# Deformable convolution on one core: window weights of upper and lower tokens stored a chunk apart in DRAM, and the last two such layers in one loop over sixteen images

## The chip, the core and the metric

The kernel runs on one core of one Trainium2 chip. The core has TensorE (PE, with a queue of its own for loading weights, PEld), VectorE (DVE), ScalarE (ACT), GpSimd (POOL) and SyncE (SP), which here issues all DMA transfers; sixteen DMA engines move the data. The metric is the device time of one execution in microseconds (us), lower is better. One execution before and one after are also profiled; every line of a profile shown here is from such an execution.

## The reference

A network of four layers over x with 8 images of 56 x 56 tokens and 128 channels, all fp32. Layers 0, 2 and 3 are deformable convolutions (DCN), each with its own weights; layer 1 is a scan over the tokens in four directions (VSS), which the change doesn't touch. A DCN layer is

```python
xp = x @ w_in + b_in
h = depthwise_conv3x3(x); h = gelu(batch_norm(h))
offset = (h @ w_off + b_off).reshape(N, H, W, GROUP, P, 2)      # GROUP = 4, P = 9
mask = softmax((h @ w_msk + b_msk).reshape(N, H, W, GROUP, P), axis=-1)
# bilinear samples of xp at 9 displaced points, a set for each group of 32 channels,
# added up with the mask as weights
y = dcn_core(xp, offset, mask) @ w_out + b_out
x = x + gamma1 * layer_norm(y, ln1_g, ln1_b)
m = gelu(x @ w_fc1 + b_fc1) @ w_fc2 + b_fc2
x = x + gamma2 * layer_norm(m, ln2_g, ln2_b)
```

## The kernel before

The sampling has no gather. The displacements of a point over one image lie in a narrow range, so all that a token samples lies in a window of fixed size around it: 14 x 11 positions in layer 0, 12 x 10 in layer 2, 15 x 14 in layer 3 (rows x columns). For each token and group of channels the kernel works out one weight for each position of the window (bilinear weight times mask, added up over the nine points), and the sampling is then a product of a matrix of weights with the rows of xp.

An image is cut into 4 row blocks of 14 rows (`rb`), each of these into 7 blocks of 14 rows x 8 columns (`q`), 112 tokens each: 28 blocks an image, 224 a layer. A layer's loop (`Dcn.loop`) goes over the blocks in order and runs several streams side by side:

- `front` makes an image ready in 43 steps: `xt` is loaded and transposed on PE (L598), xp is made (L609, added up at L610) and stored in DRAM, and from there copied into `table`, where the positions of a column of blocks with its margins (`PC` wide) lie in a row; the depthwise convolution (L631), offsets and mask (`om`), softmax, the smallest displacement of each point, which gives the addresses of L745.
- `weigh` makes the weights of a row block, two groups of channels at a time. ACT makes `hat` (Abs at L727, Relu at L729, one Abs a tap), POOL multiplies by the mask (`ay`, L733) and clears `win` (L736, four buffers), DVE makes `patch` for three points (L742, one instruction) and adds it into `win` at an address held in a register (L745, three instructions). A group's `win` (112 tokens x 7 blocks x window) is then stored to the DRAM buffer `skew`, of which there are three (`SETS`).
- `fetch` loads a block, two blocks ahead of its use. A token's weights lie in `skew` by the position in its own window, and tokens are `SA` floats apart; read with a stride of `SA - 1` between neighbouring tokens, and with `8*SA - PC` between rows, each token's weights land at their position in the block's common window. So one transfer `sw` (L755) brings, for each of the 112 tokens, one row of four groups x `SLEN` positions, zeros outside the token's own window included. The block's rows of `table` come as `xw` (L757).
- `sample` turns `sw` chunk by chunk: the `SLEN` positions are `NJ` chunks of `KP`. PE transposes the four groups of a chunk (L769) into PSUM, ACT copies them to SBUF (`st`, L771), and PE multiplies by `xw` (`products`, L780): a matmul for each group into its 32 rows of the sum `yps`. The products of a chunk are issued two chunks behind its transposes (`LAG`). In a chunk at the end of the window only the upper (0 to 63) or lower tokens (64 to 111) have anything, and only these are transposed.
- `close` copies a finished half row block to `yT` (L790). `tail`, a few steps after each block, does w_out (L804), the norms (L839 on), fc1 (L822) and fc2 (L831), with the bias as a bf16 matmul that opens the sum (L556).

The geometry of the layers:

| | layer 0 | layer 2 | layer 3 |
|---|---|---|---|
| NJ chunks x KP positions = SLEN | 4 x 128 = 512 | 4 x 112 = 448 | 5 x 120 = 600 |
| tokens turned in each chunk | 112, 112, 64, 48 | 112, 112, 56, 48 | 112, 112, 96, 48, 48 |
| SA (floats from token to token) | 2048 | 1792 | 2400 |
| floats stored for a token and group | 252 | 204 | 315 |

Order: everything that goes over a DMA queue is issued by SP in program order. Stores are put on a list (`store`) and issued behind the next `fetch` (`flush`, L568). The streams are moved on by counts in `ahead`: the next image's front is spread over 28 blocks, the weights run 6 blocks and a row block ahead.

`run` does one layer: it opens the pools, loads the layer's weights and constants (`constants`, `split_bias`), and runs the loop. The loop of the first layer starts with its first image's front and the first row block's weights, before any block; so does the loop of each later one, since a layer's loop ends with its last tail before the next one's constants. Among the steps of that first front each layer clears its DRAM buffers and their margins (`zeros`).

The pools of PSUM hold three banks for the transposes, two for `yps` and three for the rest.

Of the kernel before, what the change touches and what calls it, by code (L numbers as in the profile page):

```python
# [61 lines left out]
BR, BC = 14, 8  # L62
# [12 lines left out]

class Geo:


    def __init__(self, y0, wy, x0, wx, kx, ky):
        self.Y0, self.WY, self.X0, self.WX = y0, wy, x0, wx  # L80

        self.PC, self.HR = BC + wx - 1, 14 * -(-(H + wy - 1) // 14)
        m = (BR + wy - 1) * self.PC
        self.NJ = -(-m // 128)
        self.KP = 8 * -(-m // self.NJ // 8)
        if self.KP % 16 and self.KP != 120:
            self.KP += 8
        self.SLEN = self.NJ * self.KP

        self.chunks = []  # L90
        for j in range(self.NJ):
            top, last = j * self.KP // self.PC, ((j + 1) * self.KP - 1) // self.PC
            t0, t1 = BC * max(0, top - wy + 1), BC * min(BR, last + 1)
            self.chunks.append((j, 64 if t0 >= 64 else 0, t1))
        self.chunks.sort(key=lambda chunk: (chunk[1], -chunk[2]))
        assert self.chunks[0][1:] == (0, TB)

        self.SA = G * self.SLEN
        self.WPAD = -(-(wy * self.PC + wx - kx) // 4) * 4
# [7 lines left out]
GEO = {0: Geo(-6, 14, -6, 11, *PATCH[0]), 2: Geo(-6, 12, -5, 10, *PATCH[2]), 3: Geo(-8, 15, -7, 14, *PATCH[3])}  # L107
# [36 lines left out]
class Net:  # L144
    def __init__(self, tc, ctx, d):
# [16 lines left out]
        most = max(geo.SA for geo in GEO.values())  # L162
        self.zeros = dram("zeros", [TB, most])
        self.padded = [dram(f"padded{k}", tab) for k in range(2)]
        self.table = {x: [dram(f"table{x}{k}", [NCB * geo.HR * geo.PC + 16, C]) for k in range(3)] for x, geo in GEO.items()}
# [307 lines left out]

class Dcn:


    def __init__(self, net, layer, images, src, dst):
        self.net, self.tc, self.nc, self.d = net, net.tc, net.nc, net.d
        self.layer, self.images, self.src, self.dst = layer, images, src, dst
        self.geo = GEO[layer]  # L480
        self.KX, self.KY = PATCH[layer]
        self.table, self.skew = net.table[layer], net.skew[layer]

    def run(self):
        tc, nc = self.tc, self.nc
        with ExitStack() as ctx:
# [10 lines left out]
            self.w = self.net.dcn_weights(self.layer, self.const)  # L497
            self.constants()
            self.split_bias()
# [3 lines left out]
        with tc.If(over > 0):  # L503
            self.net.dcn_slow(self.layer, self.images, self.src, self.dst)
# [4 lines left out]
    def constants(self):  # L509
        nc, d = self.nc, self.d  # L510
        self.taps = self.const("taps", [128, 10])
        nc.sync.dma_start(out=self.taps, in_=d["c_taps"].partition_broadcast(128))
        self.lim = self.const("lim", [2 * NS, 3])
        nc.sync.dma_start(out=self.lim, in_=d[f"c_lim{self.layer}"])
        self.over = self.const("over", [2 * NS, 2])
        nc.vector.memset(self.over, 0.0)
        self.b_in = self.const("b_in_all", [128, 128])
        nc.sync.dma_start(out=self.b_in, in_=d[f"w{self.layer}_row"][0, :128].partition_broadcast(128))
        self.b_om = self.const("b_om_all", [128, OM])
        nc.sync.dma_start(out=self.b_om, in_=d[f"w{self.layer}_row"][0, 384:].partition_broadcast(128))  # L520
        pat = self.const("pat_all", [128, 2 * NS])
        nc.sync.dma_start(out=pat, in_=d["c_pat"].partition_broadcast(128))
        nc.vector.tensor_add(self.b_om[:, : 2 * NS], self.b_om[:, : 2 * NS], pat)
        self.pad = self.img.tile([128, (H + 2) * WP], F32, name="pad", tag="pad")
        nc.vector.memset(self.pad, 0.0)

# [12 lines left out]
    def split_bias(self):  # L539

        nc = self.nc
        self.ones = self.const("ones3", [3, TB], BF16)
        nc.vector.memset(self.ones, 1.0)
        self.terms = self.const("terms", [3, 2, 128], BF16)
        rest = self.w["row"][:, 128:384]
        for k in range(3):
            term = self.const(f"term{k}", [1, 256], BF16)
            nc.vector.tensor_copy(term, rest)
            nc.sync.dma_start(out=self.terms[k : k + 1].rearrange("p i c -> p (i c)"), in_=term)
            less = self.const(f"rest{k}", [1, 256])  # L550
            nc.vector.tensor_sub(less, rest, term)
            rest = less

    def bias(self, ps, i, t):

        self.nc.tensor.matmul(ps[:TB, : t * 128].rearrange("p (t c) -> p t c", c=128), lhsT=self.ones, rhs=bcast(self.terms[:, i], 1, t), start=True, stop=False)  # L556
# [13 lines left out]
    def slot(self, x, g=None, q=None):  # L570

        t, geo = self.skew[x % SETS], self.geo
        if q is None:
            return bass.AP(tensor=t.tensor, offset=t.offset + g * geo.SLEN, ap=[[geo.SA, TB], [TB * geo.SA, NCB], [1, geo.WY * geo.PC]])
# [4 lines left out]
    def front(self, i):  # L579
        nc, w, n, geo = self.nc, self.w, TB, self.geo  # L580
# [5 lines left out]
        def load(rb):  # L586
            xt = self.fp.tile([128, NT, C], F32, name="xt", tag="xt", bufs=2)
            self.last = nc.sync.dma_start(out=xt[:n], in_=self.rows_of(self.src[i], rb))
# [4 lines left out]
        for rb in range(NRB):  # L593
# [12 lines left out]
            for t0, t1 in HALVES:  # L606
# [3 lines left out]
                nc.vector.tensor_add(xp[:n, t0:t1, :], ps[:n, : 128 * (t1 - t0)].rearrange("p (t c) -> p t c", c=C), bcast(self.b_in[:n], 1, t1 - t0))  # L610
# [12 lines left out]
        for rb in range(NRB):  # L623
# [14 lines left out]
            for t0, t1 in HALVES:  # L638
# [3 lines left out]
                nc.vector.tensor_add(om[:n, NCB * rb + t0 : NCB * rb + t1, :], ps[:n, : OM * (t1 - t0)].rearrange("p (t f) -> p t f", f=OM), bcast(self.b_om[:n], 1, t1 - t0))  # L642
# [34 lines left out]
        nc.vector.tensor_scalar(base, lo, self.lim[:, 0:1], self.lim[:, 1:2], ALU.max, ALU.min)  # L677
# [7 lines left out]
        nc.vector.tensor_sub(hi, hi, self.lim[:, 2:3])  # L685
# [15 lines left out]
    def windows(self, i, c, rb=None):  # L701

        t, geo = self.table[i % 3], self.geo
# [4 lines left out]
        return t[at : at + geo.SLEN].rearrange("(j p) c -> p j c", j=geo.NJ)  # L708
# [3 lines left out]
    def weigh(self, i, rb):  # L712

        nc, n, KX, KY, geo = self.nc, TB, self.KX, self.KY, self.geo
        K, GP = max(KX, KY), 2 * NP
# [6 lines left out]
        for gg in range(0, G, 2):  # L722

            hat = self.up.tile([128, GP, NCB, 2, K], F32, name="hat", tag="hat")
# [6 lines left out]
            ay = self.up.tile([128, GP, NCB, KY], F32, name="ay", tag="ay")  # L731
            yield
            nc.gpsimd.tensor_mul(ay[:n], hat[:n, :, :, 1, :KY], bcast(m, 3, KY))  # L733
            for g in (gg, gg + 1):
                win = self.up.tile([128, NCB, geo.WPAD], F32, name="win", tag="win", bufs=4)
# [10 lines left out]
                self.store(self.slot(NRB * i + rb, g=g), win[:n, :, : geo.WY * geo.PC])  # L746
# [4 lines left out]
    def fetch(self, i, rb, q):  # L751

        nc, n, geo = self.nc, TB, self.geo
        sw = self.bp.tile([128, G, geo.SLEN], F32, name="sw", tag="sw")
        nc.sync.dma_start(out=sw[:n].rearrange("p g m -> p (g m)"), in_=self.slot(NRB * i + rb, q=q))  # L755
        xw = self.bp.tile([128, geo.NJ, C], F32, name="xw", tag="xw")
# [4 lines left out]
    def sample(self, i, rb, q, yps):  # L761

        nc, KP = self.nc, self.geo.KP
        sw, xw = self.here.pop((i, rb, q))
        for at, (j, t0, t1) in enumerate(self.geo.chunks):
            n = t1 - t0
            ps = self.pt.tile([128, 512], F32, name="pt", tag="pt")
            for g in range(G):
                last = nc.tensor.transpose(ps[:KP, n * g : n * (g + 1)], sw[t0:t1, g, KP * j : KP * (j + 1)], self.net.ident[t0:t1, t0:t1])  # L769
            st = self.bp.tile([128, G * TB], F32, name="st", tag="st", bufs=4)  # L770
            nc.scalar.copy(st[:KP, : G * n], ps[:KP, : G * n])  # L771
            self.behind.append(partial(self.products, yps, xw, st, at))
            self.catch_up(LAG, last)

    def products(self, yps, xw, st, at):
        KP = self.geo.KP
        j, t0, t1 = self.geo.chunks[at]
        n = t1 - t0
        for g in range(G):
            self.nc.tensor.matmul(yps[CG * g : CG * (g + 1), t0:t1], lhsT=xw[:KP, j, CG * g : CG * (g + 1)], rhs=st[:KP, n * g : n * (g + 1)], start=at == 0, stop=at == self.geo.NJ - 1)  # L780
# [15 lines left out]
    def tail(self, i, rb, yT, X):  # L796
        nc, w, n, net = self.nc, self.w, TB, self.net
        yT = yT.rearrange("p (n t) -> p t n", t=NT)
        parts = []
        for t0, t1 in HALVES:  # L800
            po = self.psum()
            self.bias(po, 0, t1 - t0)
# [8 lines left out]
        for t0, t1 in HALVES:  # L811
# [16 lines left out]
            self.bias(po, 1, t1 - t0)  # L828
# [7 lines left out]
        self.store(self.rows_of(self.dst[i], rb), X[:n])  # L836
# [28 lines left out]
    def loop(self):  # L865
# [4 lines left out]
        rows = [(i, rb) for i in range(self.images) for rb in range(NRB)]  # L870
# [17 lines left out]
        if self.layer not in self.net.clean:  # L888
            margins = partial(self.net.clear_margins, after=lambda: self.last)
            weights = partial(self.net.clear_weights, self.layer, after=lambda: self.last)  # L890
            zeros = {0: [margins(0)], 12: [weights(0), margins(1)], 18: [weights(1)], 42: [weights(2)]}
# [13 lines left out]
        for at, (i, rb, q) in enumerate(order):  # L905
            if q == 0:
                X = self.tp.tile([128, NT, C], F32, name="X", tag="X", bufs=3)
                nc.sync.dma_start(out=X[:TB], in_=self.rows_of(self.src[i], rb))
# [5 lines left out]
            self.sample(i, rb, q, yps[:, TB * (q - t0) : TB * (q - t0 + 1)])  # L914
# [10 lines left out]
    def all_fronts(self):  # L925

        for i in range(1, self.images):
# [494 lines left out]
def tile_net(tc, d, out, images=NIMG, layers=(0, 1, 2, 3)):  # L1422
    with ExitStack() as ctx:
        net = Net(tc, ctx, d)
        src = d["x"]
# [69 lines left out]
```

## Time and profile before

| | |
|---|---|
| median of 8 runs | 18,874.83 us (18,837.58 to 18,891.82) |
| the profiled execution, its own time and span | 18,866.81 us, span 18,865.0 us |
| granted clock of TensorE, mean | 0.802 of full speed |
| busy share of the span | PE 76%, PEld 36%, DVE 81%, ACT 60%, POOL 62% |
| layer 0, first to last block's first L769 | 170.2 to 2145.1 us |
| layer 1 | about 2160 to 14,190 us |
| layer 2, the same | 14,330.1 to 16,129.0 us |
| layer 3, the same | 16,353.1 to 18,815.8 us |
| `sw` in layers 0, 2, 3 | 896, 784, 1050 KB a block, 224 blocks each |
| L769 (transposes of `sw`) | 11,648 instructions, 1915.1 us busy, mean 302 ns of one |
| L780 (products) | 23,296 records, 1224.6 us busy, mean 296 ns |

A fp32 matmul of L780 leaves two records in the trace, a transpose of L769 one. An instruction's mean is its own duration; matmuls are pipelined, so that the distance from one's start to the next one's is shorter. In a view by stretches, "(x...)" is the number of instructions, PEclk the granted clock in that stretch and "DMA share" the mean busy share of the sixteen DMA engines. In the timeline a row is a group of like instructions with its start, busy time, and in brackets the idle time of its engine before it, with what ended that.

### The profile page before, as it was taken

What the parts mean: (1) busy time and instruction counts of PE and PEld (TensorE: products, weight loads), DVE (VectorE), ACT (ScalarE), POOL (GpSimd) and SP (SyncE); (2) the same over time, 40 slices, a digit from 0 to 9 for tenths busy, and PEclk for the clock granted to TensorE, in tenths of its full rate; (3) what the DMA queues carried; (4) which work ended last, traced back from release to release, by engine and by line L of the source; (5) the groups of instructions that cost most, each with busy time, mean ns of one, the idle gap of its engine ahead of it and who ended that gap; (6) DMA issues with size and microseconds to landing.
All of it is one profiled execution on the core that took longest, in us unless ns stands there. A gap on an engine that the chain in (4) does not pass through costs nothing. (4 is left out here: it accounts for less than half of the span.)

```text
span 18865.0 us, 237115 instructions
## 1 busy us (share of the span) xinstructions
PE 14384.4 (76%) x79747; PEld 6872.4 (36%) x79747; DVE 15318.8 (81%) x18794; ACT 11224.8 (60%) x21363; POOL 11727.3 (62%) x6462
## 2 busy tenths in 40 slices
PE   6888787678778778778778778777666888577777
PEld 4555422222222222222222222222224666455555
DVE  7777379988988988988988889888966777677776
ACT  4665555566656656666656656656554666455555
POOL 1121079988988989989989989988961122111111
PEclk6777788889888888888888888888876777666767
DMA  8888544444433333334333333333326888587777
GB/s 239 232 219 217 133 155 159 163 157 152 144 142 141 143 142 140 141 143 145 140 144 137 146 144 140 140 145 133 140 101 167 217 214 213 155 207 211 207 212 179
DMA packets 1250535, 3112.19 MB, mean 165 GB/s; under 512 B 76608, under 2 KB 868180, under 8 KB 1181468
## 3 DMA queue, kind: packets, MB, share of 16 engines
q1 hardware_dynamic: 1249292, 3096.75, 52.8%
q8 instruction: 641, 10.50, 0.2%
q14 instruction: 602, 4.93, 0.1%
HBM read 2400.54 MB, written 872.17 MB: 173 GB/s over the span
## 5 line engine op out<-in xcount | busy, mean ns | idle before, releaser
L1405 POOL TENSOR_TENSOR hc<-h,bc 128x784 f32<-128x784 f32 x4096 | 7554.4, 1872 | 1023.1 <-DVE h L1400 801.2
L1400 DVE TENSOR_TENSOR_SCAN h<-dA,st,u 128x784 f32<-128x784 f32 x3072 | 5579.0, 1839 | 384.7 <-ACT dA L1299 268.7
L1299 ACT ACTIVATE dA<-dt,v_A 128x784 f32<-128x784 f32 x4096 | 3750.0, 917 | 792.6 <-DVE h L1400 788.9
L1331 PE MATMUL acc<-hc,v_sum 128*32 128x392 f32 x16384 | 3406.9, 565 | 85.0 <-POOL hc L1405 84.7
L1309 DVE TENSOR_TENSOR u<-dtu,bc 128x784 f32<-128x784 f32 x3072 | 2887.5, 958 | 592.1 <-PE dtu L1293 475.0
L1293 PE MATMUL dtu<-dt,ident 128*128 128x392 f32 x4096 | 2091.4, 637 | 1339.9 <-issue 940.3
L769 PE MATMUL pt<-ident,sw 112*128 112x112 f32 (+8 forms) x11648 | 1915.1, 302 | 467.1 <-DMA sw<-skew 458.9
L736 POOL MEMSET win<- 128x1820 f32 (+2 forms) x384 | 631.2, 1648 | 2461.0 <-DMA skew<-win 2033.1
L1400 DVE TENSOR_TENSOR_SCAN h<-dA,st,up 128x784 f32<-128x784 f32 x1024 | 1879.9, 1836 | 260.8 <-POOL hc L1405 134.3
L771 ACT COPY st<-pt 128x448 f32<-128x448 f32 (+6 forms) x2912 | 1233.0, 444 | 1325.0 <-PE pt L769 1283.3
L1305 POOL TENSOR_TENSOR up<-dt,bc 128x784 f32<-128x784 f32 x1024 | 1905.6, 1861 | 37.5 <-DVE h L1400 30.8
L1403 ACT COPY st<-h 128x1 f32<-128x1 f32 x3072 | 584.5, 190 | 2247.8 <-DVE h L1400 2239.0
L733 POOL TENSOR_TENSOR ay<-hat,om 112x756 f32<-112x756 f32 (+2 forms) x192 | 437.3, 2278 | 2166.7 <-ACT hat L729 1905.8
L1331 PEld LDWEIGHTS acc<-hc,v_sum 128*32 128x32 f32 x16384 | 802.6, 120 | 2598.7 <-issue 1705.5
L1293 PEld LDWEIGHTS dtu<-dt,ident 128*128 128x128 f32 x4096 | 852.5, 232 | 2401.2 <-issue 1472.2
L769 PEld LDWEIGHTS pt<-ident,sw 112*128 112x128 f32 (+8 forms) x11648 | 1343.3, 172 | 1049.1 <-issue 688.4
L745 DVE TENSOR_TENSOR win<-win,patch 112x252 f32 (+2 forms) x3456 | 1574.5, 466 | 55.4 <-DVE bn_st L847 15.1
L742 DVE TENSOR_TENSOR patch<-ay,hat 112x756 f32<-112x756 f32 (+2 forms) x1152 | 1221.5, 1074 | 444.9 <-POOL ay L733 444.6
L780 PE MATMUL yps<-st,xw 120*32 120x48 f32 (+8 forms) x23296 | 1224.6, 296 | 226.9 <-ACT st L771 189.1
L1069 PE MATMUL misc<-xn,v_tap 128*128 128x448 f32 x2016 | 879.8, 581 | 117.2 <-ACT xn L1103 61.2
L822 PE MATMUL ps<-xT,w_fc 128*128 128x448 f32 (+1 forms) x1536 | 797.1, 653 | 112.6 <-ACT xT L817 74.2
L1342 ACT COPY y<-acc 64x392 f32<-64x392 f32 x768 | 577.6, 752 | 446.2 <-PE acc L1331 436.4
(163 smaller groups left out, 19396.6 us busy)
## 6 DMA issues: line engine op xcount, KB each, us to landing
dt<-dds SPq DMA_DIRECT2D x1024, 784.0 KB
bc<-rows SPq DMA_DIRECT2D x512, 784.0 KB
sw<-skew SPq DMA_DIRECT2D x224, 1050.0 KB
sw<-skew SPq DMA_DIRECT2D x224, 896.0 KB
dds<-dd SPq DMA_DIRECT2D x256, 784.0 KB
sw<-skew SPq DMA_DIRECT2D x224, 784.0 KB
skew<-win SPq DMA_DIRECT2D x128, 964.7 KB
skew<-win SPq DMA_DIRECT2D x128, 771.8 KB
```

Of the source, the lines that this page charges most:

```text
L742: nc.vector.tensor_mul(patch[:n], bcast(a, 3, KX), bcast(b, 2, KY))
L745: self.last_add = nc.vector.tensor_add(to, to, patch[:n, NCB * p : NCB * (p + 1)]).ins
L769: last = nc.tensor.transpose(ps[:KP, n * g : n * (g + 1)], sw[t0:t1, g, KP * j : KP * (j + 1)], self.net.ident[t0:t1, t0:t1])
L771: nc.scalar.copy(st[:KP, : G * n], ps[:KP, : G * n])
L780: self.nc.tensor.matmul(yps[CG * g : CG * (g + 1), t0:t1], lhsT=xw[:KP, j, CG * g : CG * (g + 1)], rhs=st[:KP, n * g : n * (g + 1)], start ...
L1293: last = nc.tensor.matmul(ps[:, b, :SH], lhsT=self.net.ident, rhs=s["dt", cg][:, 1, SH * b : SH * (b + 1)], start=True, stop=True)
L1299: nc.scalar.activation(da[:, :SC], s["dt", cg][:, 0], AF.Exp, scale=w["A"][:, k, NSG * cg + sg : NSG * cg + sg + 1])
L1305: nc.gpsimd.tensor_mul(u, s["dt", cg][:, 1], s["bc", sg][:, 0])
L1309: nc.vector.tensor_mul(halves[0], s["dtu", cg][:, :, :SH], halves[1])
L1331: nc.tensor.matmul(acc[r : r + TC, :SH], lhsT=w["sum"], rhs=hc[:, SH * b : SH * (b + 1)], start=False, stop=sg == NSG - 1)
L1400: nc.vector.tensor_tensor_scan(hh[:, ::step], dA[:, :SC][:, ::step], u[:, ::step], st[:, t : t + 1], ALU.mult, ALU.add)
L1405: nc.gpsimd.tensor_mul(hc, hh, s["bc", sg][:, 1])
```

## The change

It has two parts.

*A chunk apart.* The upper tokens (0 to 63) and the lower ones (64 to 111) of a block have common windows that lie some rows apart. The store of a group now goes out in two DMAs (`PARTS`), and the lower tokens' is written `KP` floats earlier. Read by the same skewed pattern, the lower tokens' positions then begin at the second chunk of the block's window. A row of `sw` needs fewer positions (`SLEN` 384, 336, 464 for 512, 448, 600), all chunks but none for half of the tokens: 3, 3, 4 chunks for 4, 4, 5, all of 112 tokens. `SA` becomes 1664, 1472, 1984. In `products` the upper tokens of chunk k are multiplied by chunk k of `xw` and the lower ones by chunk k+1, so that a group has two matmuls of 64 and 48 columns; since the columns of `yps` no longer all start with the same chunk, a matmul of zeros opens each half row block's sum (`open_sums`) and the products only add. `KP` is given: 128, 112, 128. A token's stored row is rounded up to 16 floats (256, 208, 320 floats).

*One loop.* `Dcn` takes a list of layers (`Part` holds what belongs to one). `tile_net` collects the layers between scans, so layer 0 runs as before by itself, and layers 2 and 3 in one loop over sixteen images, image 8 reading what layer 2 stored for image 0. Weights and constants of both layers are loaded at the start; tiles of SBUF get the larger size of the two and are used through views (`buffer`). `patch` has one buffer (before: three, in layer 3 two); `win` keeps four, `hat` and `ay` one.

```diff
+PARTS = ((0, 64), (64, TB))
...
 class Geo:
-    def __init__(self, y0, wy, x0, wx, kx, ky):
+    def __init__(self, y0, wy, x0, wx, kx, ky, kp):
...
+        self.NJ = -(-m // kp)
+        lasts = [PARTS[0][1] // BC - 1, BR - 1]
+        begin = [r * self.PC + BC - 1 - kp * h for h, r in enumerate(lasts)]
+        end = max(at + wy * self.PC - self.PC + wx for at in begin)
+        self.SLEN = 16 * -(-end // 16)
+        self.chunks = [(k, min(kp, self.SLEN - k * kp)) for k in range(-(-self.SLEN // kp))]
...
-        self.SA = G * self.SLEN
+        self.SA = G * self.SLEN + 128
+        self.WL = 16 * -(-wy * self.PC // 16)
...
-GEO = {0: Geo(-6, 14, -6, 11, *PATCH[0]), 2: Geo(-6, 12, -5, 10, *PATCH[2]), 3: Geo(-8, 15, -7, 14, *PATCH[3])}
+GEO = {0: Geo(-6, 14, -6, 11, *PATCH[0], 128), 2: Geo(-6, 12, -5, 10, *PATCH[2], 112), 3: Geo(-8, 15, -7, 14, *PATCH[3], 128)}
...
-    def slot(self, x, g=None, q=None):
+    def slot(self, x, g=None, part=None, q=None):
...
+            t0, t1 = PARTS[part]
+            return bass.AP(tensor=t.tensor, offset=t.offset + g * geo.SLEN + t0 * geo.SA - part * geo.KP, ap=[[geo.SA, t1 - t0], [TB * geo.SA, NCB], [1, geo.WL]])
...
-                    patch = self.up.tile([128, PP * NCB, KY, KX], F32, name="patch", tag="patch", bufs=3 if K < 8 else 2)
+                    patch = self.buffer("patch", (PP * NCB, KY, KX), PP * NCB * self.most(lambda p: p.KX * p.KY))
...
-                self.store(self.slot(NRB * i + rb, g=g), win[:n, :, : geo.WY * geo.PC])
+                for part, (t0, t1) in enumerate(PARTS):
+                    self.store(self.slot(NRB * i + rb, g=g, part=part), win[t0:t1, :, : geo.WL])
...
-    def sample(self, i, rb, q, yps):
+    def sample(self, i, rb, q, yps, bank):
...
+        if q in (HALVES[0][0], HALVES[1][0]):
+            self.behind.append(partial(self.open_sums, bank))
+        for k, m in geo.chunks:
             ps = self.pt.tile([128, 512], F32, name="pt", tag="pt")
             for g in range(G):
-                last = nc.tensor.transpose(ps[:KP, n * g : n * (g + 1)], sw[t0:t1, g, KP * j : KP * (j + 1)], self.net.ident[t0:t1, t0:t1])
+                p = geo.KP * k
+                last = nc.tensor.transpose(ps[:m, n * g : n * (g + 1)], sw[:n, g, p : p + m], self.net.ident[:n, :n])
...
+    def open_sums(self, bank):
+        m = bank.shape[-1] // TB
+        self.nc.tensor.matmul(bank.rearrange("p (t c) -> p t c", c=TB), lhsT=self.nought, rhs=bcast(self.ones, 1, m), start=True, stop=False)
...
-    def products(self, yps, xw, st, at):
+    def products(self, yps, xw, st, k, m, stop):
         for g in range(G):
-            self.nc.tensor.matmul(yps[CG * g : CG * (g + 1), t0:t1], lhsT=xw[:KP, j, CG * g : CG * (g + 1)], rhs=st[:KP, n * g : n * (g + 1)], start=at == 0, stop=at == self.geo.NJ - 1)
+            for part, (t0, t1) in enumerate(PARTS):
+                at = TB * g
+                self.nc.tensor.matmul(yps[CG * g : CG * (g + 1), t0:t1], lhsT=xw[:m, k + part, CG * g : CG * (g + 1)], rhs=st[:m, at + t0 : at + t1], start=False, stop=stop and part == 1)
...
-        rows = [(i, rb) for i in range(self.images) for rb in range(NRB)]
+        rows = [(i, rb) for i in range(self.images * len(self.parts)) for rb in range(NRB)]
...
-            (Vss(net, images, src, dst) if layer == 1 else Dcn(net, layer, images, src, dst)).run()
+            if layer == 1:
+                if parts:
+                    Dcn(net, images, parts).run()
+                Vss(net, images, src, dst).run()
+                parts = []
+            else:
+                parts.append((layer, src, dst))
             src = dst
+        if parts:
+            Dcn(net, images, parts).run()
```

More of the change, by code (lines that the diff above doesn't have):

```diff
@@ L887, in loop @@
         zeros = {}
[L888 to L891, printed above, removed]
+        layers = [p.layer for p in self.parts if p.layer not in self.net.clean]
+        if layers:
+            after = lambda: self.last
+            sets = [[self.net.clear_weights(layer, k, after) for layer in layers] for k in range(SETS)]
+            margins = [self.net.clear_margins(k, after) for k in range(2)]
+            zeros = {0: margins[:1], 12: sets[0] + margins[1:], 18: sets[1], 42: sets[2]}
         for k, _ in enumerate(self.front(0)):
```

173 lines of the change are left out of this document (92 added, 81 removed).

## The prediction

> **What bounds the kernel now.** I read the page first: layers 0, 2 and 3 (deformable convolution, DCN) fill the start and the last quarter, layer 1 the middle. The change leaves layer 1's loops alone, so I asked for stretches: the steady part of layer 0, 2 and 3, then the last image of layer 2 and the stretch from its last products to layer 3's first block.
>
> ```profile
> core 0: us, PE busy (x) PEld busy (x) DVE busy (x) ACT busy (x) POOL busy (x), PEclk, DMA share, GB/s
> 400.00:1900.00 1500.00, 1233.83 (x11141) 869.80 (x11139) 1126.50 (x2415) 917.83 (x1859) 291.15 (x159) 0.74 0.84 224
> 14600.00:15800.00 1200.00, 1031.17 (x9740) 730.39 (x9740) 882.37 (x2134) 772.92 (x1586) 250.15 (x144) 0.78 0.82 214
> 16800.00:18400.00 1600.00, 1256.64 (x11098) 874.71 (x11090) 1243.15 (x2078) 934.36 (x1849) 304.53 (x142) 0.69 0.78 208
> 15942.00:16130.00 188.00, 171.98 (x1728) 119.45 (x1727) 89.84 (x271) 126.05 (x273) 19.28 (x13) 0.85 0.80 200
> 16136.00:16353.00 217.00, 61.83 (x297) 50.18 (x297) 147.45 (x213) 56.12 (x90) 52.39 (x18) 0.58 0.31 93
> ```
>
> No engine is full: PE 79 to 86%, DVE 74 to 78%, the DMA engines 78 to 84%. The granted clock of 0.69 to 0.78 says that PE also stalls often. Over the seam (last row) PE works 28% of the time. The timeline shows why: the drain of one loop, then constants, a whole front, one row block of weights, their way through DRAM.
>
> ```profile
> 16136.23 3.34 PE L804 MATMUL ps<-w_out,yT 128*112 128x128 f32 x14 [0.56 <-ACT yT L790]
> ...
> 16192.48 1.54 PE L598 MATMUL ps<-ident,xt 112*128 112x112 f32 x7 [26.95 <-DMA xt<-x]
> ...
> 16353.08 2.39 PE L769 MATMUL pt<-ident,sw 112*120 112x112 f32 x12 [62.28 <-DMA sw<-skew]
> ```
>
> In the steady stretches I asked by tile what the transposes of `sw` wait for: the three lines are layers 0, 2, 3, in the windows above (us, times).
>
> ```profile
>   DMA sw<-skew: 94.0, 42
> ...
>   DMA sw<-skew: 48.3, 26
> ...
>   DMA sw<-skew: 111.5, 39
> ```
>
> The DMA view of layer 2's window says what that fetch is among all traffic: 146 x 784 KB = 117 MB of 257 MB, 46%.
>
> ```profile
> DMA packets 164504, 257.16 MB, mean 214 GB/s; under 512 B 7401, under 2 KB 136665, under 8 KB 161928
> ...
> sw<-skew SPq DMA_DIRECT2D x146, 784.0 KB
> ```
>
> By the trace's packet records (duration by packet size) the `sw` rows are dearer than their bytes: 47 to 49% of all packet time in each layer.
>
> **Part A, one loop for layers 2 and 3.** By the first L769 of each image, image 7 of layer 2 begins at 15942.1 and layer 3's first block at 16353.1: 411 us. Images 1 to 6 of layer 2 took 220 to 236 us, mean 230; image 7 is short (187 us to its last block) because no front of a next image runs beside it. In the new loop it has one, so it is an ordinary image, and its last blocks build layer 3's first weights instead of layer 2's. By DVE's rows that is 36 adds of 625 ns and 12 patches of 1545 ns (41 us) for 36 of 349 and 12 of 714 (21 us); DVE has idle time, I take 15 of the 20. So 245 us for 411: -166. The constants of two layers now load before the first front: about ten issues of 0.4 us and three more small casts with their DMAs at about 2 us each, of which I take 10 us. A = -156. Ends: if the ordinary image cost as much as one of layer 3 (316 us), -85; if the front hid wholly (187 us and the drain), -200.
>
> **Part B, the shorter rows.** `sw` goes from 896, 784, 1050 KB to 672, 588, 812 KB a block (-25, -25, -23%); other traffic changes by 2% (`skew` rows of 1024 for 1008 bytes) or 7% (`xw` of layer 3). What can be gained for certain is the wait that the tile view names. The stages last 1975, 1799 and 2463 us from first to last block, so the waits are 94.0/1500 x 1975 = 124, 48.3/1200 x 1799 = 72, 111.5/1600 x 2463 = 172: 368 us. A quarter off a transfer removes more than a quarter of the waits, as it is asked for two blocks ahead and queues behind less; each stall also costs clock afterwards. I take all of it, B = -368. Lower end: a quarter, -92. Upper end, if the DMA engines set the pace throughout: a quarter of 47% of the packet time, 12% of layers 0 and 2 and 11% of layer 3, -720; but PE and DVE stand at about 80% and would come late next, so I cap it at -600.
>
> **Part C, PE's instructions.** A block has 3 chunks for 4 (layer 3: 4 for 5), all of 112 tokens; each chunk's products split into 64 and 48 columns. Prices at full clock, from a stretch where nothing waits (start to next start):
>
> ```profile
> 16126.70 0.31 PE L780 MATMUL yps<-st,xw 112*32 112x56 f32 x8
> 16126.94 0.59 PE L769 MATMUL pt<-ident,sw 112*112 112x112 f32 x4
> 16127.47 0.29 PE L780 MATMUL yps<-st,xw 112*32 112x48 f32 x8
> 16127.69 0.42 PE L769 MATMUL pt<-ident,sw 56*112 56x56 f32 x4
> 16128.04 0.40 PE L780 MATMUL yps<-st,xw 112*32 112x112 f32 x8
> 16128.37 0.42 PE L769 MATMUL pt<-ident,sw 48*112 48x48 f32 x4
> ```
>
> Four transposes cost 0.53 (112 wide) or 0.35 us (56, 48); eight product records 0.33 (112), 0.24 (56), 0.22 (48). Layers 0 and 2 before: transposes 2 x 0.53 + 2 x 0.35 = 1.76, products 2 x 0.33 + 0.24 + 0.22 = 1.12. After: 3 x 0.53 = 1.59, and 3 x (0.25 + 0.22) = 1.41. +0.12 a block. Layer 3: 2.24 + 1.40 before, 2.12 + 1.88 after, +0.36. Times 224: 27 + 27 + 81 = 135 us. The 192 opening matmuls at L556's mean of 0.42 us add 81. Of these 216 us I put half on the path (in layer 3's chain of waits PE holds about a third, in layers 0 and 2 PE is the busiest): C = +108. Lower end 0, if the two parts overlap as four groups do; the upper end is the first rival. ACT saves some 0.15 us of copies a block, beside other work.
>
> Why eight 112-column records fit into 0.33 us: the records' starts lie 7 ns apart in fours, so the four 32-column groups run side by side, and a group's second pass starts 120 ns later. The new order issues all four passes of one group before the next group's. The Trainium skill (TensorE: Matmul & The Clock Gate, Part 3, The mechanism) says that only weight loads are pulled ahead and matmuls keep program order; by it no group would overlap the next any more, and the sum would be the first rival's. The row speaks against that rule: the first passes of four groups start before any second pass, though each group's two passes stand next to each other in the program.
>
> **Part D, the rest.** `patch` has one buffer for three (two in layer 3): DVE runs patches and adds in order itself, so only `hat` is let go later, by up to three adds; who waits for that is ACT's next `hat`, and that wait is small today. 64 half row blocks a layer x 3 adds of 0.42, 0.35, 0.625 us = 268 us is the most; I take +20. The 384 further stores cost SP 0.3 to 0.47 us each, 115 to 180 us, before the next fetches; SP mostly waits for PE, which covers it: 0, else +150.
>
> ```profile
> ACT hat L727 <- DVE patch L742: 5.9, 6, 1.4
> ...
> SPq L757 <- PE pt L769: 219.9, 56, 12.5
> ```
>
> The Trainium skill (DMA: Bandwidth & Descriptors, Rules for kernel authors) advises against two transfers for two partition halves, as they share the same DMA engines; at its fixed 2 us each, were nothing hidden, 384 would add 770 us (an estimate from that page).
>
> **Sum.** -156 - 368 + 108 + 20 = -396. The profiled execution took 18866.8 us (span 18865.0 and 1.8 around it), 8 below the median of the runs: 18,471, or 18,479 by the median; I say 18,480.
>
> **Rivals.**
> 1. Slower: PE. If a group's next pass blocks the queue, the groups no longer overlap in full. With 70 ns between passes of 48 columns and about 82 for 64, each group holds the next up for two passes, 164 ns; a chunk's products then take 3 x 0.164 + 0.39 = 0.88 us instead of the 0.36 that they cost today a chunk (815 us over the 2240 new chunks). That is +1160 us of PE. PE's idle time in the three stages is some 18% x 1975 + 14% x 1799 + 21% x 2463 = 1125; half of it can be filled. 1160 - 560 - 156 = +440, 19,310, with B swallowed. It decides from 0.68 us a chunk on. For it: the new order, and the skill's rule. Against: groups already pass each other in the records.
> 2. The wait for `sw` only changes its name. In layer 3 SP waits 503 us of 1600 for DVE's `win` before it stores, and fetches stand behind it. Then B is -92: -120, 18,750.
> 3. DMA was the pace everywhere: B = -600, 18,245. For it: DMA share 0.82 to 0.84 with `sw` at half of the packet time; against: PE's 82 to 86%.
> 4. The loops do not join, as some wait at the seam stays (registers, pools): A = 0, 18,635.
>
> **How the numbers follow.** Forecast 0.55, rivals 0.19, 0.12, 0.10, 0.04. The forecast's own range is 18,300 to 18,650 (A and B between their ends, C from 0 to 216). With rivals 2 to 4 the range is 18,230 to 18,790; rival 1 is left out. A measurement of this kernel tells about 0.2% (38 us) from no change: faster 0.77, same 0.04, slower 0.19.
>
> **What would show it.** Right: no stretch with PE under 30% between layers 2 and 3; a block's `sw` waits under a third of today's; images of layers 0, 2 and 3 at about 237, 222 and 303 us for 252, 230 and 318; clock up. C is right if a chunk's 16 product records take 0.39 to 0.5 us to the next group, and wrong from 0.68 on. The prediction is wrong if PE's busy time in these layers grows by over 500 us, or if DVE or SP lines take the place of `sw`.

## The result, and the profile after

The changed kernel takes 18,921.25 us (median of 11 runs, 18,888.88 to 18,941.14) against 18,867.79 us of the kernel before (31 runs): ratio 1.0028, 95% interval [1.0021, 1.0036]. It is slower by 53 us, where 396 us less was forecast, and lies 131 us above the forecast range. The profiled execution has a span of 18,884.3 us at a mean granted clock of 0.820 (before 0.802).

First the same stretches as before, and as the last row the seam, from layer 2's last image to layer 3's first block:

```profile
400.00:1900.00 1500.00, 1116.61 (x13027) 833.81 (x13028) 1165.08 (x2423) 904.43 (x1691) 266.56 (x163) 0.80 0.74 199
14600.00:15800.00 1200.00, 976.38 (x11393) 725.05 (x11394) 915.65 (x2138) 757.39 (x1436) 203.14 (x143) 0.82 0.71 191
16800.00:18400.00 1600.00, 1122.71 (x13109) 829.02 (x13107) 1231.06 (x1965) 877.74 (x1611) 276.63 (x134) 0.73 0.74 180
15983.00:16243.00 260.00, 200.48 (x2222) 146.70 (x2222) 195.03 (x403) 160.47 (x301) 47.88 (x28) 0.75 0.74 193
```

Columns: busy time of PE, PEld, DVE, ACT, POOL, then clock and DMA share. Much of what the forecast named is there. The DMA engines went from 0.84, 0.82, 0.78 to 0.74, 0.71, 0.74; PE is busy for less, at a higher clock; the seam has no empty stretch (PE 77%, 260 us for 411). What the transposes of `sw` wait for, by tile, in layers 0, 2 and 3 (us, times; before 94.0, 48.3 and 111.5):

```profile
  DMA sw<-skew: 33.8, 17
...
  DMA sw<-skew: 2.6, 5
...
  DMA sw<-skew: 173.4, 46
```

In layers 0 and 2 the wait fell to 36 and 5% of what it was, and the layers are no shorter; in layer 3 it grew. From the first L769 (now L810) of the first block to that of the last, with the seam from the start of layer 2's last image:

| | layer 0 | layer 2, first 7 images | seam | layer 3 |
|---|---|---|---|---|
| before | 1974.9 | 1612.0 | 411.0 | 2462.7 |
| changed | 1984.7 | 1632.8 | 260.1 | 2590.8 |

Layer 3's images 1 to 6 take 333 us for 316. That eats the seam's 151 us almost alone. A new wait stands in its place: ACT's `hat` waits for DVE's last `patch`. These are the rows of the waits of ACT in the three stretches; before, layers 0 and 2 had 13.9 and 5.9 us of it and layer 3 none:

```profile
ACT hat L764 <- DVE patch L779: 61.1, 20, 7.1
...
ACT hat L764 <- DVE patch L779: 27.2, 14, 3.1
...
ACT hat L764 <- DVE patch L779: 82.2, 17, 10.2
```

The timeline of layer 3 shows how tight it is: the last of six patches ends at 17,197.60 and the first Abs starts at 17,197.63; Relu, `ay` and the next pair's first patch follow each other.

```profile
17196.08 1.52 DVE L779 TENSOR_TENSOR patch<-ay,hat 112x1323 f32<-112x1323 f32 x1
17197.63 4.79 ACT L764 ACTIVATE hat<-om,taps 112x252 f32<-112x252 f32 x9 [4.61 <-DVE patch L779]
17202.45 2.10 ACT L766 ACTIVATE hat<-hat 112x2268 f32<-112x2268 f32 x1
17204.68 2.36 POOL L770 TENSOR_TENSOR ay<-hat,om 112x1134 f32<-112x1134 f32 x1 [10.54 <-ACT bn_rs L203]
17207.80 1.52 DVE L779 TENSOR_TENSOR patch<-ay,hat 112x1323 f32<-112x1323 f32 x1
```

I call this the ring: `hat` (one buffer) → `ay` → six patches → next `hat`. A pair of groups goes round once, eight pairs make an image. From the trace's records, means over the 9th to 56th of layer 3's 64 pairs in us (the small step from `hat` to `ay` is 0.13):

| layer 3 | hat | ay | to first patch | first to last patch | to next hat | cycle |
|---|---|---|---|---|---|---|
| before | 7.43 | 2.35 | 0.45 | 27.19 | 2.46 | 40.0 |
| changed | 7.55 | 2.34 | 0.54 | 30.96 | 0.33 | 41.8 |

Eight cycles are 335 us, an image's time, with 0.33 us of slack (the step "to next hat").

### The profile page after: what moved, and what is told of

Same layout as the page of the kernel before. It is cut to its first block, busy times and chain, and to the rows that moved or that the text cites. A ratio compares the mean times of both kernels' runs of the same rounds, so it can differ in the third digit from the quotient of the medians.

```text
span 18884.3 us, 256458 instructions
## 1 busy us (share of the span) xinstructions
PE 14029.8 (74%) x89794; PEld 6819.6 (36%) x89794; DVE 15478.7 (82%) x18787; ACT 11169.2 (59%) x20688; POOL 11619.4 (62%) x6462
## 5 line engine op out<-in xcount | busy, mean ns | idle before, releaser
L1448 DVE TENSOR_TENSOR_SCAN h<-dA,st,up 128x784 f32<-128x784 f32 x1024 | 1879.7, 1836 | 254.9 <-POOL hc L1453 126.1
L810 PE MATMUL pt<-ident,sw 112*128 112x112 f32 (+2 forms) x8960 | 1652.5, 316 | 404.1 <-DMA sw<-skew 394.0
L770 POOL TENSOR_TENSOR ay<-hat,om 112x756 f32<-112x756 f32 (+2 forms) x192 | 357.0, 1860 | 2432.7 <-ACT hat L766 1779.4
L812 ACT COPY st<-pt 128x448 f32<-128x448 f32 (+1 forms) x2240 | 1174.5, 541 | 1119.8 <-PE pt L810 1113.4
L782 DVE TENSOR_TENSOR win<-win,patch 112x252 f32 (+2 forms) x3456 | 1619.1, 468 | 131.5 <-DVE bn_st L893 21.6
L810 PEld LDWEIGHTS pt<-ident,sw 112*128 112x128 f32 (+2 forms) x8960 | 1099.8, 162 | 760.4 <-issue 324.4
L825 PE MATMUL yps<-st,xw 128*32 128x48 f32 (+5 forms) x35840 | 1116.2, 246 | 237.7 <-ACT st L812 210.3
L825 PEld LDWEIGHTS yps<-st,xw 128*32 128x32 f32 (+2 forms) x35840 | 778.6, 126 | 713.8 <-ACT st L812 297.4
L764 ACT ACTIVATE hat<-om,taps 112x252 f32<-112x252 f32 x1280 | 722.1, 720 | 353.3 <-DVE patch L779 322.6
```

Of the source, the lines that this page charges most:

```text
L782: self.last_add = nc.vector.tensor_add(to, to, patch[:n, NCB * p : NCB * (p + 1)]).ins
L810: last = nc.tensor.transpose(ps[:m, n * g : n * (g + 1)], sw[:n, g, p : p + m], self.net.ident[:n, :n])
L812: nc.scalar.copy(st[:m], ps[:m, : G * n])
L1448: nc.vector.tensor_tensor_scan(hh[:, ::step], dA[:, :SC][:, ::step], u[:, ::step], st[:, t : t + 1], ALU.mult, ALU.add)
```

## The experiments

All of them in one table: ratio to the kernel before on the same chip, and the layers from first to last block in the profiled execution. In the joined loops a front runs beside layer 2's last image, so its layer 2 is longer by that. In the three kernels without a ratio the sums of layer 0 are made from the wrong weights, displacements of later layers leave the window and the slow path (`dcn_slow`) runs, outside the stretches read (31 to 44 ms in all); only their stages are read. A stage is one profiled execution, so that a few us between two kernels tell nothing.

| kernel | ratio [95%] | layer 0 | layer 2 | layer 3 |
|---|---|---|---|---|
| before | 1 | 1974.9 | 1798.9 | 2462.7 |
| changed | 1.0028 [1.0021, 1.0036] | 1984.7 | 1872.0 | 2590.8 |
| e2 skew only | 0.9966 [0.9952, 0.9979] | 1968.4 | 1798.9 | 2394.0 |
| e3 changed, patch buffers back | 0.9915 [0.9901, 0.9928] | 1977.0 | 1879.7 | 2407.9 |
| e4 before, one patch buffer | 1.0261 [1.0247, 1.0275] | 2108.4 | 1883.9 | 2676.9 |
| e5 merge only, one patch buffer | 1.0210 [1.0196, 1.0224] | 2126.9 | 1928.7 | 2693.3 |
| e6 changed, two hats | 0.9893 [0.9878, 0.9908] | 1993.1 | 1885.2 | 2358.0 |
| e7 e2 with two hats and ays | 0.9959 [0.9945, 0.9973] | 1997.0 | 1805.3 | 2358.5 |
| e9 e3, two adds of three | 0.9861 [0.9846, 0.9876] | 2000.7 | 1846.1 | 2373.7 |
| e8 e3, half of sw, own order | | 1820.9 | 1745.4 | 2367.7 |
| e10 e3, all of sw, e8's order | 0.9872 [0.9857, 0.9887] | 1898.5 | 1816.8 | 2441.2 |
| e11 half of sw, e3's order | | 1976.4 | 1881.8 | 2364.0 |
| e12 e3 in the changed kernel's order | 1.0005 [0.9995, 1.0014] | 1970.0 | 1871.5 | 2594.5 |
| e13 e6 in the order for half of sw | 0.9835 [0.9822, 0.9849] | 1869.1 | 1872.4 | 2346.5 |
| e14 before, half of sw, same order | | 1908.5 | 1775.5 | 2322.8 |

**First set: which part costs.** Theory 1 was the single patch buffer, theory 2 that the fetch was never the bound.

e2, the weights a chunk apart alone:

```diff
-                parts.append((layer, src, dst))
+                Dcn(net, images, [(layer, src, dst)]).run()
...
-PP * NCB * self.most(lambda p: p.KX * p.KY))
+PP * NCB * self.most(lambda p: p.KX * p.KY), 3 if K < 8 else 2)
```

> Only the stored weights a chunk apart (shorter rows, two stores, 64/48 columns, opening matmul); loops of layers 2 and 3 apart as before, and patch keeps three buffers (two in layer 3). Theory 1, the single patch buffer holds hat and with it the weights back and ate the gain: about 18,570 us (-300), the waits of the sw transposes gone and no more DVE wait for ay than before (445 us). Theory 2, the fetch never bounded the loop, the wait only moves to the making of the weights: 18,870 within 60, with PE waiting longer for h, X and q in place of sw.

0.34% less, 64 us of 18,868: nearer to theory 2 for the transfer (-300 expected by theory 1). Layers 0 and 2 gained 6.5 and 0 us, layer 3 gained 69. In layers 0 and 2 no wait of the transposes for `sw` is left in the same windows, where 94.0 and 48.3 us stood before; in layer 3 it is 19.9 for 111.5. The waits went, and in layers 0 and 2 the time did not.

e3, the changed kernel with its patch buffers back:

```diff
-PP * NCB * self.most(lambda p: p.KX * p.KY))
+PP * NCB * self.most(lambda p: p.KX * p.KY), 3 if len(self.parts) == 1 else 2)
```

> The changed kernel with patch given back its buffers: three in layer 0, two in the joined loop. Theory 1: about 18,480 to 18,600, layer 3's images near 303 us. Theory 2: as the changed kernel, 18,880 to 18,940, since the merge has its gain already and the patches were not what is late.

0.85% less than before, between the two expectations, and 1.13% or 213 us less than the changed kernel, nearly all in layer 3 (310 us an image for 333). So one line of the change, the buffer count, costs 213 us. The rest of the change is worth -160, where its steps said -416.

e4, one patch buffer and nothing else, in the kernel before:

```diff
-tag="patch", bufs=3 if K < 8 else 2)
+tag="patch", bufs=1)
```

> The kernel before with one patch buffer in all three layers and nothing else. Theory 1: slower by 200 to 350 us, 19,070 to 19,220, layer 3 most (16 us an image), with DVE waiting longer for ay and ACT's hat for patch. Theory 2: within 60 us of before.

+2.61%, 490 us, above either expectation: 64 x 3 adds a layer (268 us), the most that the prediction allowed, are not the mechanism.

e5, the joined loop alone: in the changed kernel the geometry, the stores, `sample` and `products` are again those of before.

```diff
-for part, (t0, t1) in enumerate(PARTS):
-    self.store(self.slot(NRB * i + rb, g=g, part=part), win[t0:t1, :, : geo.WL])
+self.store(self.slot(NRB * i + rb, g=g), win[:n, :, : geo.WY * geo.PC])
...
-self.SA = G * self.SLEN + 128
+self.SA = G * self.SLEN
```

> The kernel before with the last two layers in one loop and one patch buffer (two did not fit into SBUF), the skewed weights as before. The seam should give some 130 to 156 us in any case. Theory 1: about 18,870 - 145 + 270 = 19,000. Theory 2: about 18,725.

+2.10%: against e4 the join is worth -0.51%, 96 us; e3 against e2 gives the same 0.51%. The total of 19,000 was missed since e4's price was.

**Second set: the ring.** If the ring sets the pace, a second `hat` opens it even with one patch buffer.

```diff
-hat = self.buffer("hat", (GP, NCB, 2, K), GP * NCB * 2 * self.most(lambda p: max(p.KX, p.KY)))
+hat = self.buffer("hat", (GP, NCB, 2, K), GP * NCB * 2 * self.most(lambda p: max(p.KX, p.KY)), 2)
```

> The changed kernel, patch still with one buffer, but two buffers for hat (constants' scratch is put into one of them, before the loop). Ring theory: a pair of groups goes hat (ACT), ay (POOL), patches (DVE), and the next hat waits for the last patch since hat has one buffer; in the changed kernel's layer 3 these add up to 41.8 us a pair, 8 pairs an image, 335 us, with 0.3 us of slack. With two hats only ay and patches are left in the ring (34 us), so layer 3 falls to about 310 us an image and the whole to about 18,710. Order theory: one patch buffer makes DVE's fixed order bad, whatever hat has: 18,880 to 18,940.

0.9893, as the ring theory said (0.992): layer 3's images fall from 333 to 302 us, while layers 0 and 2 get 8 and 13 us longer. In layer 3 still no patch stands ahead of the adds of the one before it, but the next `hat` now starts 30 us before the last patch ends, where it came 0.33 us behind. This fits a single patch buffer that costs by closing the ring through the single `hat`; it doesn't show it alone, since the second buffer also changed the order of the instructions on DVE and ACT (more on that below).

e7, which is e2 with two buffers each for `hat` and `ay`:

```diff
-GP * NCB * 2 * self.most(lambda p: max(p.KX, p.KY)))
+GP * NCB * 2 * self.most(lambda p: max(p.KX, p.KY)), 2)
...
-GP * NCB * self.most(lambda p: p.KY))
+GP * NCB * self.most(lambda p: p.KY), 2)
```

> Loops of layers 2 and 3 apart, weights a chunk apart, patch with three (layer 3: two) buffers, and two each for hat and ay. Ring theory: nothing of a pair waits for the pair before it, so layer 3 (308 us an image with one hat) falls below 300 and the whole by 60 to 200 from the 18,800 of the skewed weights alone; layers 0 and 2, with 5 us of slack in the ring, by less. If the ring only follows something else: 18,800 within 40.

0.9959 against 0.9966 of e2: nothing, though layer 3 fell by 36 us (to 305 an image, where under 300 was expected); layer 0 rose by 29. Opening the ring thus helps layer 3, by 233 us in e6 and 36 in e7, and layers 0 and 2 in neither. Here too the order changed with the buffers.

e9, a third of DVE's adds left out of e3:

```diff
-for p in range(PP):
+for p in range(PP - 1):
     to = win[:n, :, bass.ds(...
```

> The changed kernel with its patch buffers back (18,707), with two of the three adds of each patch (the third point's weights are left out of win). DVE does 1152 adds less, 536 us of its time. Ring theory: layer 3, whose ring is tight, gains 6 x 0.625 us a pair, up to 240 us; layers 0 and 2 at most a little: 18,450 to 18,600. If DVE is not in the pace: 18,707 within 40.

536 us of DVE's time are gone and 0.54%, 102 us, are won; layer 3 gains 34, layer 2 34, layer 0 loses 24. Outside both expectations: a cut of DVE's work gives a fifth of its time. Whether DVE's time would count in e3's own order stays open, since leaving out the adds also changed the order on DVE and ACT.

e8, half the bytes of `sw`, in e3:

```diff
-nc.sync.dma_start(out=sw[:n].rearrange("p g m -> p (g m)"), in_=self.slot(NRB * i + rb, q=q))
+nc.sync.dma_start(out=sw[:n, : G // 2].rearrange("p g m -> p (g m)"), in_=self.slot(NRB * i + rb, q=q, groups=G // 2))
...
-last = nc.tensor.transpose(ps[:m, n * g : n * (g + 1)], sw[:n, g, p : p + m], self.net.ident[:n, :n])
+last = nc.tensor.transpose(ps[:m, n * g : n * (g + 1)], sw[:n, g % 2, p : p + m], self.net.ident[:n, :n])
```

> The changed kernel with its patch buffers back (18,707), and each sw row fetched for two of the four groups only; the transposes of groups 2 and 3 read those of 0 and 1, so that everything but the bytes of sw stays (the sampled sums are those of other weights). If the fetch still sets the pace of these layers: 150 us or more below 18,707. Ring theory: less than 60, in layer 3 alone, where sw is waited for 95 us of 1400.

Layers 0, 2, 3 fall by 156, 134 and 40 us: this seemed to bring the transfer back as the bound. But e3 does not wait for `sw` in layer 0: the answer that names what the transposes wait for has no row for `sw` there. Comparing the two programs settled what else differs. Both hold the same instructions, and the order on each engine is worked out at build time by a scheduler that goes by estimated durations; with `sw` half as long, only 14% of DVE's and 11% of PE's instructions of layer 0's block stand at the same place. Most moved by little: half of them by at most 9 places of 8240 on DVE and 13 of 10,747 on PE. e8 had changed two things.

**Third set: order against bytes.** So the order was taken out of the scheduler's hands. In e10 and e11 every instruction gets an edge "issued behind" to the one that stands before it on its engine in a written-out list; all else is as in e3 and e8. In the traces DVE and ACT run the same instructions in the same order in e11 as in e3, and in e10 as in e8, over layer 0.

```diff
         tile_net(tc, aps, out)
+        pin(tc, nc)
...
+        for k in names[rank]:
+            now = here.get(f"I-{k}")
...
+            if last is not None and last[1] == now[1]:
+                tc.add_manual_dep(now[0], last[0].name, edge, reason="pin")
+            last = now
```

> The kernel with patch buffers back (18,707), all of sw fetched, but every queue's instructions pinned to the order that the scheduler chose when it saw sw rows of half the length. With half the bytes and that order layers 0, 2 and 3 took 1821, 1745 and 2368 us from first to last block, against 1977, 1880 and 2408 with all bytes and their own order. Order theory (the order, which the scheduler works out from the sizes, sets the pace): near 1821, 1745, 2368, a total of about 18,380 to 18,450. Bytes theory (sw's transfer still sets the pace): near 1977, 1880, 2408, about 18,680 to 18,730, or slower for an order that expects its data sooner.

> The other corner: sw for two of four groups only (the sampled sums are those of other weights), in the order that belongs to all four. Order theory: layers 0, 2, 3 near 1977, 1880, 2408 us from first to last block. Bytes theory: near 1821, 1745, 2368. Read by the stages, not by the total.

With e8 and e3 this makes a square (us from first to last block):

| | layer 0: all / half of sw | layer 2 | layer 3 |
|---|---|---|---|
| e3's order | 1977.0 / 1976.4 | 1879.7 / 1881.8 | 2407.9 / 2364.0 |
| e8's order | 1898.5 / 1820.9 | 1816.8 / 1745.4 | 2441.2 / 2367.7 |

In the order that e3 has, half the bytes are worth 0.6 us in layer 0, nothing in layer 2, and 44 us in layer 3. With all bytes the other order alone takes off 78 and 63 us (and adds 33 in layer 3). Only in that order do the bytes count in layers 0 and 2, by 78 and 71 us, and in layer 3 by 74. Neither theory held alone: in layers 0 and 2 the order says whether the transfer is felt, in layer 3 it is felt in both. Layer 0, the stretch from 400 to 1900 us, one row for each kernel (columns as above). e3, its own order and all bytes:

```profile
400.00:1900.00 1500.00, 1160.86 (x13119) 859.32 (x13119) 1166.66 (x2425) 901.58 (x1695) 270.15 (x161) 0.79 0.73 198
```

e11, e3's order and half the bytes:

```profile
400.00:1900.00 1500.00, 1156.50 (x13123) 858.28 (x13124) 1168.95 (x2425) 901.93 (x1698) 269.70 (x162) 0.80 0.56 161
```

e10, the other order and all bytes:

```profile
400.00:1900.00 1500.00, 1165.80 (x13561) 863.12 (x13563) 1164.14 (x2502) 931.20 (x1751) 295.88 (x166) 0.81 0.75 204
```

From e3 to e11 the DMA share falls from 0.73 to 0.56, and the stretch holds the same number of instructions, 13,119 and 13,123 on PE. In e10 it holds 13,561. And e10, the faster one, is the one that waits for `sw`, where e3 does not at all (its transposes by tile, same stretch):

```profile
  DMA sw<-skew: 94.9, 48
```

So the longer wait for `sw` stands in the faster kernel: when the order lets PE arrive sooner, PE waits longer. There the wait also has a price: over layer 0 it is 94.9/1500 x 1898.5 = 120 us, of which half the bytes took off 78.

e12 asks the same of the patch buffer: e3, which has the buffers, pinned (the edit as above, with another list) to the order of the changed kernel.

> Patch with three buffers in layer 0 and two in the joined loop, as in the kernel of 18,707, but every queue pinned to the order of the changed kernel, which has one. If the single buffer costs by its order (patches no longer pulled ahead of adds, so hat is let go late): as the changed kernel, 18,900 to 18,940. If it costs by waits of the hardware for the buffer: 18,707 to 18,760.

Layer 3 takes 2594.5 us, the changed kernel's 2590.8. The ratio of 1.0005 lies 0.90% or 170 us above e3, out of the 213 that the changed kernel lies above it. So most of the single buffer's cost is what it does to the order; at most the other 43 us are waits for the buffer itself. Counted in the traces, in the kernel before 72% of the patches of layer 3 stand ahead of adds of the patch before them, in e3 also 72%, in e4, e12 and the changed kernel none. With the patches pulled ahead, `hat` is let go sooner: from first to last patch it is 26.57 us a pair in e3, 31.00 in e12 (a cycle of 38.8 against 41.85). With 0.92 us of slack, e3's ring in layer 3 is nearly closed too.

e13 puts two hats and another order together: e6, pinned to the order that it gets with `sw` half as long.

> The changed kernel with two buffers for hat (18,713), pinned to the order that the scheduler chose for it with sw rows of half the length, all of sw fetched. Order theory: another order of the same work moves the time by one per cent or more, here down, to about 18,400. Bytes theory: 18,713 within 40.

0.9835: 0.58% below e6 with the same instructions, 1.65% below the kernel before (some 310 us), the fastest here. It was expected lower (0.975); layer 0 gave 124 us, the others 13 and 12.

e14 goes back to the kernel before, pinned to its own order, with half of `sw` as in e8, to see whether the waits named there were worth their time.

> The kernel before, sw fetched for two of the four groups only (the sampled sums are those of other weights), every queue pinned to the order of the kernel before. Its layers 0, 2 and 3 took 1975, 1799 and 2463 us from first to last block. If the prediction's premise of part B held, that the waits named sw are time to be won, half the bytes take at least the 124, 72 and 172 us off: near 1850, 1727 and 2290. Order theory: the order holds the pace, the wait goes to the next name: within 30 us of 1975 and 1799, and at most 60 below 2463.

Layers 0, 2 and 3 fall by 66, 23 and 140 us, 229 in all: in layers 0 and 3 between the two expectations, in layer 2 as the order theory said. Of PE's waits in layer 0 (us, times, longest) these are the rows before:

```profile
PE pt L769 <- DMA sw<-skew: 85.7, 37, 6.0
PE yps L780 <- ACT st L771: 43.9, 37, 4.5
```

In e14 the wait for `sw` fell, and that for the copies of `st` rose:

```profile
PE yps L780 <- ACT st L771: 73.6, 46, 7.4
...
PE pt L769 <- DMA sw<-skew: 18.8, 11, 4.8
```

So in this order half the bytes bring 62% of the 368 us named (53, 32 and 81% in layers 0, 2 and 3), and that is a cut of the bytes twice the change's.

## Why the prediction was wrong

Forecast -396, measured +53: 449 us are missing. By steps, with e2, e3 and the changed kernel (64 = 0.34%, 96 = 0.51%, 213 = 1.13% of 18,868):

**Part A, -156, got -96.** The mechanism was right, and the seam nearly to size: layer 2's last image to layer 3's first block is 260 us for 411, where 245 were said. Between the profiled executions of e2 and e3, which lie 75 us apart, the seam gives 396 to 257, -139, where -166 was said; about 11 us go to the longer constants (10 were said). The rest the prediction put at nothing: 30 us to the seven images of layer 2 before the seam, 14 to layer 3, 6 to layer 0. In layer 2 the joined loop has two patch buffers for three and another order; which of them costs was not tried. 60 us missing.

**Parts B and C, -260 together, got -64.** The step that failed is "I take all of it". A wait named in the profile is time only if nothing else is as late, and e14 says 229 us for twice the cut. With the shorter rows came a new order, in which the transfer is not felt at all in layers 0 and 2 (e11): in e2 the waits for `sw` there are gone, and of the 124 and 72 us that they were priced at 6.5 and 0 were won. I had the upper end at -600 from the DMA engines' load and the lower at -92; both took the rest of the program as fixed. How much of e2's 64 us is bytes and how much order stays open: e2 and the kernel before have different instructions, so one can't be pinned to the other.

C itself came out better than said, as a term. In the timeline of the changed layer 2 a chunk's 16 product records start, and the next instruction starts 0.36 us later, which is also the median of the 1762 such chunks, where +108 rested on 0.47 (and the sign for C began at 0.39); with three transposed chunks for four PE's busy time fell (1233.8 to 1116.6 us of 1500 in layer 0):

```profile
16107.84 0.60 PE L810 MATMUL pt<-ident,sw 112*112 112x112 f32 x4
16108.36 0.42 PE L825 MATMUL yps<-st,xw 112*32 112x64 f32 x16
16108.72 0.59 PE L810 MATMUL pt<-ident,sw 112*112 112x112 f32 x4
```

**Part D, +20, got +213.** This step failed in its premise, "DVE runs patches and adds in order itself". The kernel's text has that order, DVE's queue had another. The scheduler had pulled 72% of the patches ahead, which three and two buffers allow and one does not. The bound of 268 us counted the adds that let `hat` go later; e4's 490 us lie above it, so more than these adds stands in the way, presumably whatever else DVE does between the patches. The row to be read was in the profile before: ring 40.0 us a pair, 2.46 of slack. 193 us missing; A, B with C and D make the 449. The 384 further stores, which were put at 0 (+150 if SP's other waits don't cover them, 770 by the estimate with nothing hidden), are in e2 too, which is 64 us faster than before: no cost of that size shows.

**Rivals.** Rival 1 is refuted by the timeline above: 0.36 us, where it decides from 0.68 on. The Trainium skill (TensorE: Matmul & The Clock Gate, Part 3, The mechanism), from whose rule the prediction worked out 0.88, is not borne out by these rows. Rival 2 was nearest in kind: the wait changed its name, in layer 3 to the place it gave (SP's wait for `win` before a store, 503 us of 1600 before, 588 after). But it stopped at -120. Rival 3, -600 for a quarter of the bytes, is refuted by e14's 229 us for half of them, in the order of the kernel before. Rival 4 is refuted by the seam. Only rival 1 had the sign, with a mechanism that isn't there; none took the order as a thing that the change changes. Of what was to show the prediction wrong, "DVE or SP lines take the place of sw" is what came.

## What to carry to other kernels

Where a scheduler orders each engine's instructions by estimated durations, a change of a size or of a buffer count can be a change of order, as it was in these runs, and that alone moved this kernel by -0.6% to +0.9% with the same instructions. Compare the two programs' orders engine by engine before pricing a change, and count what a buffer lets the scheduler pull ahead. Look for rings: a single buffer that is passed round three engines, with its parts added up against the time of an iteration; where the sum is the iteration, that loop is worth opening (e6: 233 us of layer 3). Such a ring does not make other waits free: in e3's layer 3, with 0.92 us of slack, half the bytes still gave 44 us. Nor does a named wait that goes away bring its time: check what is as late behind it. To split bytes or buffers from order, pin the order and change one of them.

## What the runs showed of the hardware

PE's groups of 32 columns overlapped in the new order as in the old: 16 records of two passes and two parts a group take 0.36 us to the next instruction, against 0.33 for 8 records of 112 columns before. In 1760 of 1762 such chunks all eight records of 64 columns start (in the median 0 to 120 ns behind the first) before the eight of 48 (136 to 219 ns), though the program puts a group's two parts next to each other. In e3's order, taking the DMA engines' share from 0.73 to 0.56 changed layer 0 by 0.6 us. And longer, rounder rows were not cheaper to store: by the packet records a 1260 B row of `skew` took 65 ns in layer 3 and one of 1280 B 91 ns (77 in e2), one of 1008 B 53 ns in layer 0 and one of 1024 B 62 ns (59 in e2); why was not tried.
